# The last 64 channels of convolution and gate, made for two chunks at once in the column halves of the array

## The chip, the cores and the metric

The kernel runs on one core of one Trainium2 chip. The metric is the time of one execution in device microseconds. Durations of single operations come from one profiled execution; the other executions were timed without a profile.

## The reference

Four layers work on `x`, float32, 4 images of 96 channels, 64 x 64 pixels. Layer 0 is a state-space block; the change lies in its first part:

```python
xn = _ln(xp, in_norm_g, in_norm_b)              # tokens of 96 channels
proj = xn @ in_proj_w.T                         # 96 -> 2 * 192
xq, z = jnp.split(proj, 2, axis=-1)
z = _silu(z)                                    # the gate, 192 channels
xc = depthwise_conv_3x3(xq, conv_w)             # 192 channels, 'SAME'
xc = _silu(xc + conv_b)
xs = four directions of xc                      # rows, columns, both flipped
dts, Bs, Cs = split(einsum('bkdl,kcd->bkcl', xs, x_proj_w))
y = selective_scan(xs, dt_proj(dts), A, Bs, Cs, Ds, dt_b)    # 192 channels x 16 states
y = _ln(sum of the four directions of y) * z
x = x + y @ out_proj_w.T
```

Layer 1 is a deformable 3 x 3 convolution (offsets and masks from two convolutions, bilinear samples), layer 2 a Fourier mixer and an MLP with float8 products, layer 3 linear attention and an MLP of the same kind.

## The kernel before

**The scan.** An image is 4096 tokens, cut into 8 chunks of 512 (`CH`, `NCH`). Layer 0's scan runs over units: an image, a direction k, a step of 1024 tokens (two chunks), and 8 channels with their 16 states on the 128 partitions. That makes 1536 units. Each unit has a decay on ScalarE (`decay`, L1014), two bf16 matmuls on TensorE that spread the inflow over the states (`inflow`, L1020), a product on VectorE (L1034), the scan on VectorE (`recur`, L1042), a product on GpSimd (`weigh`, L1051), and its share of a sum over states on TensorE (`total`, L1070). The spread of a unit is issued one unit ahead of its scan, its decay two, the loads of `da` five units ahead (on ScalarE's queue); `du` and `bc` are loaded by SP (L1009, L1000).

**The streams beside it.** All other work is written as generators that yield a `Step` with an estimated time on each engine. `Net`, `Clock`, `pipe` and `Stream` put these steps between the units: a step is issued when the planner's clock says that the engines it needs have room. This happens while the program is built; each engine then has a fixed order of instructions, and at run time waits only for semaphores. There are two streams. The first, `ends`, prepares image 0 (`first`), images 1, 2 and 3 (`before`), and then does layers 2 and 3 image by image (`image`). The second, `middle`, finishes layer 0 behind the scan (`behind`) and does layer 1 with its gathers, also image by image, and is asked first. An image of layers 2 and 3 starts when its samples are there (`net.sampled`). The matmuls of both streams share three PSUM banks (`net.mm`, pool `mm`) while the scan has its own.

**The convolution.** `prepare` multiplies the depthwise weights into the projection, so that a tap of the convolution is a matmul from 96 input channels, over a window of the padded, normed image `pad` that is shifted by the tap. `conv` (L750) makes one chunk: nine taps into one PSUM bank for channels 0 to 127 (g = 0), then nine taps for channels 128 to 191 (g = 1). The second has only 64 channels, so its 64 weight columns stand twice in `w_in` and in the taps' weights, and the sum appears on both halves of the partitions. ScalarE takes the sum through Silu: into `xa` for g = 0 (L773); for g = 1 the lower half into `xc[:64]` in row order (L775), and the upper half into `xc[64:]` in column order (L776). Two gate matmuls follow (L787), for channels 0 to 127 and for 128 to 191, where only 64 of 128 columns are of use; Silu puts them into `zt` (L789), and SP stores z and u (L794 to L796). Silu and the exponential lie in different tables of ScalarE; `exp_and_log` (L411) reloads the latter after each use of Silu.

In `first` (L610) the convolution of chunk j+1 goes beside the projection and the discretisation of chunk j (`projected`, `steps`), in a pipe of six chains; these need the tag `c{j}`, which chunk j's convolution frees when it ends. For images 1 to 3, `inputs` (L690) runs the eight chunks' convolutions in a pipe of two chains, and the rest follows in `before` (L650). `zt` has one buffer for each of its tags; the tag `zt` in the pipe lets one chain at a time be in the gate.

Of the kernel before, what the change touches and what calls it, by code (L numbers as in the profile page):

```python
# [8 lines left out]
F32 = mybir.dt.float32  # L9
# [5 lines left out]
AF = mybir.ActivationFunctionType  # L15
# [539 lines left out]
class Layer0:  # L555
# [54 lines left out]
    def first(self):  # L610
# [5 lines left out]
        with tc.tile_pool(name=f"l0u{b}", bufs=1) as up, tc.tile_pool(name=f"l0b{b}", bufs=1) as sm:  # L616
# [5 lines left out]
            with tc.tile_pool(name=f"l0a{b}", bufs=1) as big, tc.tile_pool(name=f"l0i{b}", bufs=1) as cp:  # L622
# [4 lines left out]
                def rows_first():  # L627
                    yield self.conv(b, 0, pad, us, weights, cp)
                    for j in range(NCH):
                        if j + 1 < NCH:  # L630
                            yield self.conv(b, j + 1, pad, us, weights, cp)
                        yield self.projected(b, j, us, xp_a, xp_c, sm, xdbl, (0,), f"c{j}")
                        for ks in ((0,), (0, 2), (2,)):
                            yield self.steps(b, ks, j, us, dtw, sm, xdbl)
# [55 lines left out]
    def inputs(self, b, up, us):  # L690
# [3 lines left out]
        with tc.tile_pool(name=f"l0a{b}", bufs=1) as big:  # L694
            pad = big.tile([C, PW, PW], F32, name=f"pad{b}", tag="pad")
            yield from self.normed_rows(b, x, pad)
            with tc.tile_pool(name=f"l0i{b}", bufs=1) as sm:
                weights = self.conv_weights(b, sm)
                yield wait(4.0)
                yield from pipe(  # L700
                    self.net, (self.conv(b, j, pad, us, weights, sm) for j in range(NCH)), 2,
                    zt=1, **{f"c{j}": 0 for j in range(NCH)},
                )

# [42 lines left out]
        nc.sync.dma_start(wz, self.net.ins["w_in"][:, 256:])  # L747
        return wc, wz

    def conv(self, b, j, pad, us, weights, sm):  # L750

        net, rows, as_rows = self.net, self.rows, self.as_rows
        nc = net.nc
        wc, wz = weights
        xa, _, xc = us
        xct_v = xc.rearrange("p (w h) -> p h w", h=H)
        cs = slice(j * CH, (j + 1) * CH)
        r0 = j * NR
        for g in range(2):
            pp = net.mm(f"pc{g}_{b}_{j}")  # L760
            for q in range(9):
                dy, dx = divmod(q, 3)
                nc.tensor.matmul(  # L763
                    pp,
                    lhsT=wc[:, q, g * 128 : (g + 1) * 128],
                    rhs=pad[:, r0 + dy : r0 + dy + NR, dx : dx + W],
                    start=(q == 0),
                    stop=(q == 8),
                )
                if q < 8:  # L770
                    yield cost(pe=0.8, holds=1)
            if g == 0:
                nc.scalar.activation(xa[:, cs], pp, AF.Silu, bias=net.vec(V_CBA))  # L773
            else:
                nc.scalar.activation(xc[:64, cs], pp[:64], AF.Silu, bias=net.vec(V_CBC, 64))  # L775
                nc.scalar.activation(  # L776
                    xct_v[64:, r0 : r0 + NR, :],
                    as_rows(pp[64:]),
                    AF.Silu,
                    bias=net.vec(V_CBC, 64, 64),  # L780
                )
            net.exp_and_log()
            yield cost(pe=0.8, act=4.0, new=True, takes="zt" if g else "")
        zts = []
        for g, (c0, n) in enumerate(((0, 128), (128, D2))):
            pz = net.mm(f"pz{g}_{b}_{j}")
            nc.tensor.matmul(pz, lhsT=wz[:, c0 : c0 + 128], rhs=rows(pad, j), start=True, stop=True)  # L787
            zt = sm.tile([128, CH], F32, name=f"zt{g}_{b}_{j}", tag=f"zt{g}")
            nc.scalar.activation(zt[:n], pz[:n], AF.Silu)  # L789
            zts.append((c0, n, zt))  # L790
        net.exp_and_log()
        yield cost(pe=2.0, act=3.8)
        for c0, n, zt in zts:
            nc.sync.dma_start(self.z_d[b][c0 : c0 + n, cs], zt[:n])  # L794
        nc.sync.dma_start(self.u_d[b][:128, cs], xa[:, cs])
        nc.sync.dma_start(self.u_d[b][128:, cs], xc[:64, cs])  # L796
        yield wait(frees=f"zt c{j}")

    def projected(self, b, j, us, xp_a, xp_c, sm, xdbl, qs, takes=""):

# [1120 lines left out]
```

## Time and profile before

| | |
|---|---|
| median of 3 timed executions | 8629.55 us (8617.16 to 8655.84) |
| profiled execution | 8600.48 us |
| its span, first to last instruction | 8598.7 us |
| mean granted TensorE clock | 0.785 of full speed |
| VectorE busy | 6817.9 us (79%) |
| TensorE busy | 6553.4 us (76%) |
| GpSimd busy | 5626.7 us (65%) |
| ScalarE busy | 4945.4 us (58%) |
| first scan starts, last scan ends | 184.97 us, 7551 us |
| convolution's taps (L763) | 568.7 us busy, 1152 records, from 63 to 3588 us |
| gate's matmuls (L787) | 128 records |
| ScalarE's table loads | 201, of 1283 ns each |

In the lines of the profile an entry names the engine (PE is TensorE, PEld its weight load, DVE VectorE, ACT ScalarE, POOL GpSimd, SP the engine that issues most DMAs), the source line, and the tiles written and read. `<-` in a wait names what ended it. A float32 matmul appears as two records. Matmuls are pipelined, so the distance from start to start tells their cost better than their durations. The chain of waits is followed back from the last instruction; here it ends at 3137 us.

### The profile page before, as it was taken

What the parts mean: (1) busy time and instruction counts of PE and PEld (TensorE: products, weight loads), DVE (VectorE), ACT (ScalarE), POOL (GpSimd) and SP (SyncE); (2) the same over time, 40 slices, a digit from 0 to 9 for tenths busy, and PEclk for the clock granted to TensorE, in tenths of its full rate; (3) what the DMA queues carried; (4) which work ended last, traced back from release to release, by engine and by line L of the source; (5) the groups of instructions that cost most, each with busy time, mean ns of one, the idle gap of its engine ahead of it and who ended that gap; (6) DMA issues with size and microseconds to landing.
All of it is one profiled execution on the core that took longest, in us unless ns stands there. A gap on an engine that the chain in (4) does not pass through costs nothing.

```text
span 8598.7 us, 97186 instructions
## 1 busy us (share of the span) xinstructions
PE 6553.4 (76%) x31960; PEld 2840.7 (33%) x31960; DVE 6817.9 (79%) x5118; ACT 4945.4 (58%) x9071; POOL 5626.7 (65%) x4308
## 2 busy tenths in 40 slices
PE   6775877689767668777767888777788776897587
PEld 2211221122222223311223555223455331464374
DVE  2799989888799888688898888888887887838714
ACT  5664666556567668755666667554567765333224
POOL 1565667566579788665688888665787886527700
PEclk8766877779677779876777888676788887798698
DMA  3677678868779889876888989766898887744420
GB/s 97 166 198 195 169 196 220 210 166 201 182 216 243 220 230 226 204 193 181 209 228 223 230 230 229 169 163 166 229 228 226 204 216 180 180 104 137 143 63 13
DMA packets 773932, 1608.32 MB, mean 187 GB/s; under 512 B 264081, under 2 KB 355757, under 8 KB 771222
## 3 DMA queue, kind: packets, MB, share of 16 engines
q10 hardware_dynamic: 244224, 843.17, 38.9%
q1 hardware_dynamic: 455478, 532.37, 24.0%
q0 software_dynamic: 73728, 226.57, 10.1%
q8 instruction: 256, 4.19, 0.2%
q14 instruction: 246, 2.02, 0.1%
HBM read 1345.43 MB, written 256.29 MB: 186 GB/s over the span
## 4 chain that ended last, share of the span: by engine, by line
PE 27%; DVE 14%; DMA 7%; ACT 7%; issue 4%; POOL 2%; ACTq 1%; SPq 1%; DVEq 0%; POOLq 0%
DVE hh L1042 7%; DVE db L1034 3%; PE ps L1416 3%; PE f L1510 3%; PE py L1070 3%; DMA da<-de 2%; PE pd L1432 2%; ACT g L1395 2%; PE db L1020 2%; ACT da L1014 1%; PE h L1551 1%; PE yp L1590 1%; PE zp L1576 1%; POOL hh L1051 1%; PE py L1065 1%
## 5 line engine op out<-in xcount | busy, mean ns | idle before, releaser
L1051 POOL TENSOR_TENSOR hh<-hh,bc 128x1024 f32<-128x1024 f32 x1536 | 3672.1, 2393 | 354.9 <-DVE hh L1042 225.1
L1042 DVE TENSOR_TENSOR_SCAN hh<-da,st,db 128x1024 f32<-128x1024 f32 x1152 | 2700.9, 2345 | 209.5 <-PE py L1070 79.8
L1034 DVE TENSOR_TENSOR db<-db,bc 128x1024 f32<-128x1024 f32 x1536 | 1864.0, 1214 | 610.2 <-PE db L1020 608.7
L1014 ACT ACTIVATE da<-da,w_al 128x1024 f32<-128x1024 f32 x1536 | 1737.6, 1146 | 476.8 <-DMA da<-de 129.9
L1383 POOL DMA_INDIRECT g<-table,idx x1152 | 1201.7, 1043 | 372.3 <-issue 174.8
L1020 PE MATMUL db<-du,rep 24*128 24x512 bf16 x3072 | 700.5, 457 | 780.1 <-DVE hh L1042 748.9
L1070 PE MATMUL py<-hh,w_fold 128*32 128x512 f32 x6144 | 1120.5, 792 | 35.4 <-POOL hh L1051 19.3
L1395 ACT ACTIVATE g<-g,wt 128x96 f32<-128x96 f32 x3456 | 968.3, 364 | 116.7 <-PE py L1070 30.7
L1042 DVE TENSOR_TENSOR_SCAN hh<-da,db 128x1024 f32<-128x1024 f32 x384 | 877.2, 2284 | 73.2 <-PE py L1070 25.1
L1416 PE MATMUL ps<-w_ident,g 128*96 128x128 f32 x3744 | 688.8, 329 | 222.8 <-issue 90.6
L1020 PEld LDWEIGHTS <-rep 24*128 24x128 bf16 x3072 | 159.5, 94 | 1909.3 <-issue 1228.5
L851 POOL TENSOR_TENSOR lw<-lw,w 128x512 f32<-128x512 f32 x192 | 244.0, 1271 | 718.0 <-DVE w L849 686.0
L1416 PEld LDWEIGHTS ps<-w_ident,g 128*96 128x96 f32 x3744 | 499.4, 148 | 568.6 <-ACT g L1395 176.7
L1049 POOL COPY st<-hh 128x1 f32<-128x1 f32 x1152 | 235.1, 204 | 685.3 <-DVE hh L1042 650.5
L763 PE MATMUL pc<-pad,wc 96*128 96x512 f32 x1152 | 568.7, 630 | 6.9 <-ACT st L1424 2.6
L1424 ACT COPY st<-ps 96x384 f32<-96x384 f32 x384 | 180.1, 472 | 543.6 <-PE ps L1416 506.0
L882 PE MATMUL pr<-ex,w_ident 128*128 128x512 f32 x384 | 294.7, 859 | 147.6 <-DVE ex L872 58.6
L840 PE MATMUL pd<-xd,w_dtw 103*64 103x512 f32 (+1 forms) x512 | 279.0, 820 | 68.1 <-DVE rl L853 30.4
L1432 PE MATMUL pd<-st,wdc 96*128 96x256 f32 x1152 | 320.5, 430 | 11.4 <-ACT st L1424 4.8
L763 PEld LDWEIGHTS pc<-pad,wc 96*128 96x128 f32 x1152 | 217.1, 199 | 308.7 <-issue 289.2
L1070 PEld LDWEIGHTS py<-hh,w_fold 128*32 128x32 f32 x6144 | 160.5, 125 | 387.4 <-issue 293.6
L1519 ACT COPY d<-f 128x512 f32<-128x512 f32 x192 | 111.2, 581 | 299.7 <-PE f L1510 287.5
(253 smaller groups left out, 8940.0 us busy)
## 6 DMA issues: line engine op xcount, KB each, us to landing
da<-de ACTq DMA_DIRECT2D x1536, 512.0 KB
du<-du SPq DMA_DIRECT2D x1536, 96.0 KB
bc<-bcd SPq DMA_DIRECT2D x128, 512.0 KB
y<-yb SPq DMA_DIRECT2D x384, 128.0 KB
de<-rl SPq DMA_DIRECT2D x128, 256.0 KB
m<-in_dft SPq DMA_DIRECT2D x128, 256.0 KB
ad<-y ACTq DMA_DIRECT2D x192, 128.0 KB
table<-pix SPq DMA_DIRECT2D x256, 96.0 KB
```

Source lines behind the costliest of these rows:

```text
L763: nc.tensor.matmul(pp, lhsT=wc[:, q, g * 128 : (g + 1) * 128], rhs=pad[:, r0 + dy : r0 + dy + NR, dx : dx + W], start=(q == 0), stop=(q == 8),
L882: nc.tensor.matmul(pr, lhsT=net.ident, rhs=ex, start=True, stop=False)
L1014: self.net.nc.scalar.activation(u.da, u.da, AF.Exp, scale=self.al[:, a : a + 1])
L1020: self.net.nc.tensor.matmul(db[:, h, :], lhsT=self.rep[64 * u.q + 32 * h : 64 * u.q + 32 * h + 24], rhs=u.du[64 * u.q + 32 * h : 64 * u.q ...
L1034: self.net.nc.vector.tensor_mul(u.db, u.db, u.bc[:, 0, :])
L1042: nc.vector.tensor_tensor_scan(u.along(u.hh), u.along(u.da), u.along(u.db), first, ALU.mult, ALU.add)
L1051: self.net.nc.gpsimd.tensor_mul(u.hh, u.hh, u.bc[:, 1, :])
L1070: nc.tensor.matmul(py[p0 : p0 + 32], lhsT=self.fold[:, u.i, :], rhs=hc[:, h * CH : (h + 1) * CH], start=u.sums["add"] is None and u.i == 0 ...
L1383: nc.gpsimd.indirect_dma_start(out=g[:, k, :], out_offset=None, in_=self.tables[b % 2], in_offset=bass.IndirectOffsetOnAxis(ap=idx[:, n : ...
L1395: nc.scalar.activation(pixel, pixel, AF.Identity, scale=wt[:, n, c : c + 1])
L1416: nc.tensor.matmul(pt[:, k, :], lhsT=g[:, k, c * C : (c + 1) * C], rhs=net.ident, is_transpose=True, start=(c == 0), stop=(c == corners - 1),)
L1432: nc.tensor.matmul(po, lhsT=wdc[:, k, :], rhs=st[:, k, :], start=(k == 0), stop=(k == 8))
```

## The change

`conv` now makes a pair of chunks. The 128-channel part is done as before, for one chunk and then for the other. For the last 64 channels the weights are used once: each tap is two matmuls with 64 columns, the first chunk's sum on partitions 0 to 63 and the second chunk's on 64 to 127 of the same bank, that is, one in each column half of the array. Two activations then read each half, one for the row order and one for the column order. The gate's last 64 channels are made in the same way, and one activation takes both halves. The planner's costs of these steps are changed with it, `first` and `inputs` count pairs, the second chunk's gate has a tile of its own, and both chunks' tags are freed together. Their z and u are stored in one group of eight DMAs.

```diff
@@ first
                 def rows_first():
                     yield self.conv(b, 0, pad, us, weights, cp)
                     for j in range(NCH):
-                        if j + 1 < NCH:
-                            yield self.conv(b, j + 1, pad, us, weights, cp)
+                        if j % 2 == 0 and j + 2 < NCH:
+                            yield self.conv(b, j // 2 + 1, pad, us, weights, cp)
@@ inputs
-                    self.net, (self.conv(b, j, pad, us, weights, sm) for j in range(NCH)), 2,
+                    self.net, (self.conv(b, jp, pad, us, weights, sm) for jp in range(NCH // 2)), 2,
@@ conv
-    def conv(self, b, j, pad, us, weights, sm):
+    def conv(self, b, jp, pad, us, weights, sm):
 
         net, rows, as_rows = self.net, self.rows, self.as_rows
         nc = net.nc
         wc, wz = weights
         xa, _, xc = us
         xct_v = xc.rearrange("p (w h) -> p h w", h=H)
-        cs = slice(j * CH, (j + 1) * CH)
-        r0 = j * NR
-        for g in range(2):
-            pp = net.mm(f"pc{g}_{b}_{j}")
+        pair = (2 * jp, 2 * jp + 1)
+        key = f"{b}_{jp}"
+
+        def shifted(j, q):
+            dy, dx = divmod(q, 3)
+            return pad[:, j * NR + dy : j * NR + dy + NR, dx : dx + W]
+
+        for j in pair:
+            pp = net.mm(f"pc0_{b}_{j}")
             for q in range(9):
-                dy, dx = divmod(q, 3)
                 nc.tensor.matmul(
-                    pp,
-                    lhsT=wc[:, q, g * 128 : (g + 1) * 128],
-                    rhs=pad[:, r0 + dy : r0 + dy + NR, dx : dx + W],
+                    pp, lhsT=wc[:, q, :128], rhs=shifted(j, q), start=(q == 0), stop=(q == 8)
+                )
+                if q < 8:
+                    yield cost(pe=0.8, holds=1)
+            nc.scalar.activation(xa[:, j * CH : (j + 1) * CH], pp, AF.Silu, bias=net.vec(V_CBA))
+            net.exp_and_log()
+            yield cost(pe=0.8, act=2.0, new=True)
+        pp = net.mm(f"pc1_{key}")
+        for q in range(9):
+            for i, j in enumerate(pair):
+                nc.tensor.matmul(
+                    pp[64 * i : 64 * i + 64],
+                    lhsT=wc[:, q, 128:192],
+                    rhs=shifted(j, q),
                     start=(q == 0),
                     stop=(q == 8),
                 )
-                if q < 8:
-                    yield cost(pe=0.8, holds=1)
-            if g == 0:
-                nc.scalar.activation(xa[:, cs], pp, AF.Silu, bias=net.vec(V_CBA))
-            else:
-                nc.scalar.activation(xc[:64, cs], pp[:64], AF.Silu, bias=net.vec(V_CBC, 64))
-                nc.scalar.activation(
-                    xct_v[64:, r0 : r0 + NR, :],
-                    as_rows(pp[64:]),
-                    AF.Silu,
-                    bias=net.vec(V_CBC, 64, 64),
-                )
-            net.exp_and_log()
-            yield cost(pe=0.8, act=4.0, new=True, takes="zt" if g else "")
+            if q < 8:
+                yield cost(pe=0.8, holds=1)
+        for i, j in enumerate(pair):
+            half, bias = pp[64 * i : 64 * i + 64], net.vec(V_CBC, 64, 64 * i)
+            nc.scalar.activation(xc[:64, j * CH : (j + 1) * CH], half, AF.Silu, bias=bias)
+            nc.scalar.activation(xct_v[64:, j * NR : (j + 1) * NR, :], as_rows(half), AF.Silu, bias=bias)
+        net.exp_and_log()
+        yield cost(pe=0.8, act=4.2, new=True, takes="zt")
         zts = []
-        for g, (c0, n) in enumerate(((0, 128), (128, D2))):
-            pz = net.mm(f"pz{g}_{b}_{j}")
-            nc.tensor.matmul(pz, lhsT=wz[:, c0 : c0 + 128], rhs=rows(pad, j), start=True, stop=True)
-            zt = sm.tile([128, CH], F32, name=f"zt{g}_{b}_{j}", tag=f"zt{g}")
-            nc.scalar.activation(zt[:n], pz[:n], AF.Silu)
-            zts.append((c0, n, zt))
+        for j in pair:
+            pz = net.mm(f"pz0_{b}_{j}")
+            nc.tensor.matmul(pz, lhsT=wz[:, :128], rhs=rows(pad, j), start=True, stop=True)
+            zt = sm.tile([128, CH], F32, name=f"zt{j % 2}_{b}_{j}", tag=f"zt{j % 2}")
+            nc.scalar.activation(zt, pz, AF.Silu)
+            zts.append(zt)
+        pz = net.mm(f"pz1_{key}")
+        for i, j in enumerate(pair):
+            nc.tensor.matmul(
+                pz[64 * i : 64 * i + 64], lhsT=wz[:, 128:192], rhs=rows(pad, j), start=True, stop=True
+            )
+        zc = sm.tile([128, CH], F32, name=f"zt2_{key}", tag="zt2")
+        nc.scalar.activation(zc, pz, AF.Silu)
         net.exp_and_log()
-        yield cost(pe=2.0, act=3.8)
-        for c0, n, zt in zts:
-            nc.sync.dma_start(self.z_d[b][c0 : c0 + n, cs], zt[:n])
-        nc.sync.dma_start(self.u_d[b][:128, cs], xa[:, cs])
-        nc.sync.dma_start(self.u_d[b][128:, cs], xc[:64, cs])
-        yield wait(frees=f"zt c{j}")
+        yield cost(pe=3.0, act=4.5)
+        for i, j in enumerate(pair):
+            cs = slice(j * CH, (j + 1) * CH)
+            nc.sync.dma_start(self.z_d[b][:128, cs], zts[i])
+            nc.sync.dma_start(self.z_d[b][128:, cs], zc[64 * i : 64 * i + 64])
+            nc.sync.dma_start(self.u_d[b][:128, cs], xa[:, cs])
+            nc.sync.dma_start(self.u_d[b][128:, cs], xc[:64, cs])
+        yield wait(frees=f"zt c{pair[0]} c{pair[1]}")
```

## The prediction

> **What bounds the kernel now.** I read the page first, then busy times by stretch, VectorE's waits, the convolution's own lines, the chain of waits in one convolution stage, and the order in time around one pair of half-width matmuls.
>
> The first scan (L1042) starts at 184.97 us and the last ends at 7551: 1536 units of 4.8 us. Before lie image 0's norm and first chunks, behind lie 1048 us of image 3's last stages. Stretches (columns: busy us of each engine, TensorE clock, DMA): the scan phase, and the convolutions of images 1, 2 and 3.
>
> ```profile
> core 0: us, PE busy (x) PEld busy (x) DVE busy (x) ACT busy (x) POOL busy (x), PEclk, DMA share, GB/s
> 185.00:7551.00 7366.00, 5617.16 (x25964) 2244.70 (x25964) 6275.75 (x4295) 4532.11 (x8308) 5243.82 (x3981) 0.77 0.80 203
> ...
> 940.00:1150.00 210.00, 195.55 (x628) 68.65 (x632) 183.38 (x106) 149.95 (x146) 128.08 (x82) 0.95 0.73 186
> 1840.00:2150.00 310.00, 283.03 (x886) 87.38 (x884) 261.88 (x162) 193.93 (x206) 199.85 (x135) 0.92 0.82 196
> 3300.00:3600.00 300.00, 271.95 (x1164) 118.44 (x1160) 228.08 (x134) 258.25 (x507) 234.25 (x180) 0.96 0.86 221
> ```
>
> Over the whole phase VectorE is busiest (6276 of 7366, 85%). In the three convolution stages it is TensorE: 93%, 91%, 91%, VectorE 87%, 84%, 76%. VectorE's idle time in the scan phase (last two numbers: times, longest):
>
> ```profile
> DVE db L1034 <- PE db L1020: 584.4, 278, 29.1
> DVE hh L1042 <- PE py L1070: 104.9, 98, 5.9
> DVE hh L1042 <- ACT da L1014: 29.6, 20, 3.8
> ```
>
> So TensorE late with the spread inflow is what VectorE waits for. In image 3's stage (3290 to 3610) the chain of waits runs over the convolution; it is traced back to 3137 us only, so the earlier stages can't be read so.
>
> ```profile
> by line: PE pc L763 22.8%; PE ps L1416 8.3%; ACT g L1395 7.9%; DVE hh L1042 7.3%; ACT da L1014 6.9%; PE py L1070 5.8%; PE pd L1432 5.4%; ACT L413 4.4%; issue 4.2%; DVE db L1034 3.8%; PE db L1020 3.7%; DMA wc<-wc_d 3.1%; PE py L1065 2.8%; AC
> ```
>
> 22.8% of 320 us is 73 us of taps, and 4.4% is 14 us of reloading the exponential table (L413). The price of a pair of half-width matmuls, in order of time (start, us):
>
> ```profile
> 137.48 3.60 PE L763 MATMUL pc<-pad,wc 96*128 96x512 f32 x8
> 140.91 1.02 PE L882 MATMUL pr<-ex,w_ident 128*128 128x512 f32 x2
> ...
> 143.07 1.88 PE L763 MATMUL pc<-pad,wc 96*128 96x512 f32 x4
> 144.97 1.08 PE L840 MATMUL pd<-xd,w_dtw 103*64 103x512 f32 x4
> 145.98 1.55 PE L763 MATMUL pc<-pad,wc 96*128 96x512 f32 x3
> ```
>
> One fp32 matmul is two records. Eight records take 140.91-137.48 = 3.43 us from start to start, so 0.86 us a matmul: call that a slot. The two 64-column matmuls of `pd`, in different column halves, take 145.98-144.97 = 1.01 us together, not 1.72; they overlap. The four records before them take 1.90 instead of 1.72. Going into half columns and out again so costs 0.18+0.15 = 0.33 us.
>
> **What the Trainium skill says.** "TensorEngine Tiling (Array Packing)", Key Properties: tiles of one mode run independently, but a change of mode drains TensorE. The trace agrees with both (1.01 us for two; 0.33 us a change). "TensorE: Matmul & The Clock Gate", Part 3, table of measured speedups: three column tiles of 32 gave 2.38 times. Here the offset convolution, over the same shifted windows, does better with four: 18 matmuls (36 records) in 5.28 us are 0.29 us each, 2.9 times.
>
> ```profile
> 7651.46 5.28 PE po L1278 x36
> ```
>
> "ScalarE: Activation LUTs", What ACT_TABLE_LOAD costs: 1283 ns, and 1380 ns of drain. The loads are 1.283 us here, but the next instruction follows at once (an activation ends at 72.01, load at 72.02, next load at 73.31), so I count no drain. "PSUM — Partial Sum Buffer", Engine vs sequencer instructions: matmuls start and end in program order; so a matmul waiting for a bank holds all behind it. The same bears on the last rival below.
>
> **The change, part by part, for a pair of chunks** (16 pairs).
>
> *TensorE.* Before: 36 tap and 4 gate matmuls, 40 slots, 34.4 us. After: 18 taps of 128 channels, 9 slots of two half-width taps, 2 gates and 1 shared gate slot, 30 slots, 25.8 us: 8.6 us less. In the order of the changed program the half-width taps stand in 46 runs and the shared gates in 16; 62 changes of 0.33 us are 20 us, 1.3 us a pair. Left: 7.3 us a pair, 117 us in all.
>
> *ScalarE.* Before: 12 table loads of 1.283 (15.4 us), 2 x 0.687 + 2 x 0.682 + 2 x 1.145 + 4 x 0.590 = 7.4 us. After: 8 loads (10.3 us), one gate activation less (6.8 us). 5.7 us a pair, 91 us in all.
>
> *VectorE, GpSimd, DMA.* Same operations, same bytes. The eight stores of z and u leave in one go behind the last gate; SP waited 226 us for the gate before (36 times), now half as often and longer. Behind it on SP stand the scan's du and bc loads, which are issued at least five units (some 24 us) before their use; eight issues of about 0.5 us are covered. If that cover went, each of twelve groups could cost what exceeds it: 0 to 5 us, so 60 us at most. I take 0.
>
> *Before the first scan.* Projection of chunk 0 stands behind 48 slots instead of 41 (+6 us); from there to the first spread there are 30 instead of 39 convolution slots (-8 us) and 44 instead of 51 us of ScalarE work. I take 0, bounds -8 and +8. But 42 slots are left for the scan phase instead of 80.
>
> *Planned order.* The planner's cost of a half-width step is still 0.8 us for two overlapping taps. So convolution 1 stands beside units 146-173 instead of 151-194, convolution 3 beside 579-628 instead of 650-706, and image 3's last preparation at unit 795 instead of 889. Fourier and MLP work of image 1 then ends at unit 1426, not 1473; image 2 can't follow, since its samples come at unit 1472 in both orders. So half the lead is spent waiting, VectorE's total work beside the scan is the same, and the 1048 us behind the scan are the same work in the same order.
>
> *What that is worth, by stage.* Four pairs save 29 us of TensorE an image. Image 3: VectorE has room (228 of 300); of the 80 us of taps and gates on the chain 7.3/34.4 go, 17 us, and a quarter of the 32 us of ScalarE's convolution work on it, 8: 25 us. Image 2: room too, VectorE 262 of 310: 18 us. Image 1: 183 of 210 is nearly VectorE's limit, 12 us. Image 0: 156 us from 185 to 341, where VectorE is busy 107 and TensorE 117: mostly latencies, 10 us of the 33 us that leave. Sum 65; of this I give back 10 for the wait at unit 1426, where the scan runs a little quicker but has nothing to fill. **-55 us.** A second way: cutting the scan phase into stretches of 16 units and fitting their length to the work of TensorE and VectorE in them gives 0.27 us per us of TensorE and 0.97 per us of VectorE: 134 us of slots less are then -41 with an error of 15. I keep -55, since these fits mix stages where TensorE has room.
>
> **Rivals.**
>
> *VectorE is the bound, and TensorE's time goes idle.* For it: 85% busy over the phase; in the convolution stages the waits for `db` are no denser than elsewhere. Against it: 91 to 93% TensorE there and the chain. Time: 0 to -15 us, 8615 to 8630.
>
> *The halves don't overlap, or the changes of mode eat the gain.* Then 40 slots as before, planned as 30: -0, and late spreads, say 8640. Against it: 1.01 us for two.
>
> *The gate takes its banks in one step, and it gets slower.* The pool has three banks; the changed gate step asks for three at once (two before), while the half-width sum is still being read (1.28 + 2 x 1.83 = 4.9 us) and the other chain holds a third bank. TensorE then stands until ScalarE has read the sum, reloaded (1.28), loaded (1.28) and copied the first gate (0.59); the next unit's spread is queued behind. The inflow is one unit early, so the first 4 us are covered. To come out slower by 0.5% each of 16 pairs must cost VectorE (55+43)/16 = 6 us. For it: ScalarE's queue also carries decays and sampling. Against it: all waits of the gate's matmuls now are about 70 us for 64. Where it decides, +60 us: 8690. Another order of everything beside the scan, with its chances both ways (a stretch of 16 units scatters by 8 us around the fit), belongs to the range.
>
> **How the numbers follow.** The profiled execution took 8600.48 us, 1.8 more than its span; the median of the runs shown is 8629.55, 0.34% more, so 55 us stay 55. 8629.55-55 = **8575**. Chances: the forecast 0.55 (own range 8535 to 8610; 0.46 of it beyond 0.5%, below 8586, and 0.09 short of it), VectorE's bound 0.20 (no change), no overlap 0.05 (0.03 none, 0.02 slower), gate 0.20 (0.03 none, 0.17 slower). About 0.5% is what a measurement tells here from no change: 8617 to 8656 is the scatter. Faster 0.46, same 0.35, slower 0.19. Range 8500 to 8690: the planner's reshuffle below, the gate above.
>
> **What would show it.** Half-width taps: pairs start 0.86 to 0.9 us apart inside a run. ScalarE busy about 91 us less, TensorE 100 to 120. First scan at 177 to 193. Convolution stages with VectorE above 88%. Last scan near 7500, 1048 us behind it unchanged. If the gate's matmuls wait for ScalarE by over 100 us in all, or spreads make VectorE wait by more than 584 us, the last rival holds. Wrong altogether if the scan's units outside the convolution stages change their pace.

## The result, and the profile after

The changed kernel takes 8689.4 us, median of 20 executions (8652.27 to 8724.51); the kernel before, run beside it, 8638.25 us (20 executions). The ratio is 1.0059, 95% interval 1.0045 to 1.0073: slower by 0.6%, where 0.6% faster was forecast. The profiled execution's span is 8659.5 us, its mean granted TensorE clock 0.773 (before: 8598.7 us, 0.785).

The first section of the page, busy time of each engine, of the kernel after:

```profile
PE 6445.4 (74%) x31938; PEld 2783.5 (32%) x31960; DVE 6814.1 (79%) x5118; ACT 4855.5 (56%) x8991; POOL 5606.8 (65%) x4308
```

Against 6553.4 and 4945.4 us before, TensorE works 108 us less (99 to 134 between the two profiles taken of each kernel) and ScalarE 90 us less, nearly what was forecast (100 to 120, and 91). So the work did leave. In the stretches view the scan phase comes first, then the convolutions of images 1, 2 and 3, each from the first chunk's activation into `xa` to the last chunk's:

```profile
core 0: us, PE busy (x) PEld busy (x) DVE busy (x) ACT busy (x) POOL busy (x), PEclk, DMA share, GB/s
192.00:7565.00 7373.00, 5495.84 (x25930) 2181.56 (x25952) 6273.52 (x4296) 4447.62 (x8233) 5235.82 (x3981) 0.76 0.79 203
938.00:1074.00 136.00, 123.20 (x416) 38.28 (x414) 94.72 (x55) 85.51 (x85) 68.06 (x51) 0.90 0.60 161
1743.00:1930.00 187.00, 177.77 (x597) 50.22 (x595) 145.89 (x89) 114.90 (x124) 117.33 (x92) 0.90 0.74 191
3085.00:3314.00 229.00, 203.38 (x877) 78.51 (x877) 171.66 (x101) 175.52 (x344) 176.08 (x151) 0.88 0.82 214
```

The scan phase is as long as before (7373 against 7366 us) with the same VectorE time in it (6274 against 6276). The convolutions are over sooner, but VectorE is busy in only 70, 78 and 75% of them, against 87, 82 and 75% in the same stretches of the kernel before (its second profile, `before_again` below): they now stand beside 27, 39 and 48 scan units instead of 43, 62 and 57. TensorE fills 91, 95 and 89% of these shorter stages, at a granted clock of about 0.9, so the time that left it was not filled with scan units. In the chain of waits over image 3's stage (3060 to 3340 us) the taps (L767 and L778) still make 20.4% of 280 us, 57 us, against 73 before:

```profile
by line: PE pc L767 11.7%; PE pc L778 8.7%; DMA da<-de 8.0%; PE ps L1434 7.8%; ACT g L1413 7.6%; PE py L1088 6.6%; PE pd L1450 6.4%; DVE hh L1060 6.0%; PE db L1038 4.8%; PE py L1083 4.5%; issue 3.6%; ACT L413 3.2%; ACTq L1011 3.0%; ACT da L
```

VectorE's waits (total, times, longest) answer the three lines of before:

```profile
DVE db L1052 <- PE db L1038: 575.4, 251, 23.2
...
DVE hh L1060 <- PE py L1088: 93.6, 83, 5.0
...
DVE hh L1060 <- ACT da L1032: 13.0, 16, 1.9
```

The wait for the spread (`db`) is 575 us where it was 584: no difference for the whole (the second profiles of both kernels have 599 and 596), but in units 144 to 192, where image 1's convolution lies, it is 53 us in the changed kernel and 14 before. What is new is in TensorE's own waits, at the shared gate (L802):

```profile
PE pz L802 <- ACT zt L798: 46.6, 10, 7.2
...
PE pz L802 <- ACT xa L772: 4.8, 2, 2.6
```

In order of time (start, us; in brackets the wait just ahead of it), two groups of full-width matmuls for comparison, two runs of half-width taps of image 1, and the gate that follows:

```profile
935.97 1.98 PE L767 MATMUL pc<-pad,wc 96*128 96x512 f32 x4
...
942.16 1.07 PE L1088 MATMUL py<-hh,w_fold 128*32 128x512 f32 x8
...
952.06 3.65 PE L778 MATMUL pc<-pad,wc 96*64 96x512 f32 x16
...
955.96 4.51 PE L778 MATMUL pc<-pad,wc 96*64 96x512 f32 x20
...
961.72 1.13 PE L767 MATMUL pc<-pad,wc 96*128 96x512 f32 x2
...
963.10 2.31 PE L796 MATMUL pz<-pad,wz 96*128 96x512 f32 x4
964.25 1.28 ACT L413 ACT_TABLE_LOAD   x1
965.54 2.19 ACT L1032 ACTIVATE da<-da,w_al 128x1024 f32<-128x1024 f32 x2
967.75 1.28 ACT L798 ACT_TABLE_LOAD   x1
969.04 1.08 ACT L798 ACTIVATE zt<-pz 128x512 f32<-128x512 f32 x2
969.69 1.98 PE L802 MATMUL pz<-pad,wz 96*64 96x512 f32 x4 [4.28 <-ACT zt L798]
971.60 3.78 PE L767 MATMUL pc<-pad,wc 96*128 96x512 f32 x4
...
975.32 0.60 PE L1038 MATMUL db<-du,rep 24*128 24x512 bf16 x2
975.85 1.94 PE L1088 MATMUL py<-hh,w_fold 128*32 128x512 f32 x8
977.71 2.58 PE L767 MATMUL pc<-pad,wc 96*128 96x512 f32 x4
```

The half-width taps do overlap: 20 records are ten matmuls, five pairs, 0.89 us a pair from start to start. Then two plain gate matmuls take two banks at 963.10. The next pair's taps hold the third (L767 at 961.72, sum not finished), so the shared gate can only have the bank of the first gate matmul, and that is read only after a reload of the exponential table, two decays and the load of Silu's table: the first of the two copies at 969.04 ends about 969.6, and TensorE starts 0.1 us later, having stood 4.28 us, in which no other matmul ran. After that it is slow: four records take 3.78 us (1.98 at 935.97), eight of `py` 1.94 (1.07 at 942.16). From start to start the work from 969.69 to 980.22 is about 4.4 us longer than at the usual pace, so this wait takes twice its length of TensorE. "TensorE: Matmul & The Clock Gate", Part 1, says the clock falls to half after an idle window of about 3.4 us; the trace agrees here: its record of the granted clock stands at half from 968.70 us, 3.3 us into the wait, for 10.24 us. (`third_bank` below shows that less is enough.)

### The profile page after: what moved, and what is told of

It reads as the page before. It is cut to its first block, busy times and chain, and to the rows that moved or that the text cites. A ratio compares the mean times of both kernels' runs of the same rounds, so it can differ in the third digit from the quotient of the medians.

```text
span 8659.5 us, 97118 instructions
## 1 busy us (share of the span) xinstructions
PE 6445.4 (74%) x31938; PEld 2783.5 (32%) x31960; DVE 6814.1 (79%) x5118; ACT 4855.5 (56%) x8991; POOL 5606.8 (65%) x4308
## 4 chain that ended last, share of the span: by engine, by line
PE 35%; DVE 30%; DMA 11%; ACT 9%; issue 8%; POOL 2%; ACTq 1%; SPq 1%; another core or an unknown queue 0%; DVEq 0%; POOLq 0%
DVE hh L1060 15%; DVE db L1052 8%; PE py L1088 4%; PE ps L1434 4%; DMA da<-de 3%; PE f L1528 3%; PE pd L1450 3%; PE pc L767 2%; ACT g L1413 2%; PE db L1038 2%; ACT da L1032 2%; PE py L1083 1%; PE pc L778 1%; ACTq L1011 1%; POOL hh L1069 1%
## 5 line engine op out<-in xcount | busy, mean ns | idle before, releaser
L1434 PE MATMUL ps<-w_ident,g 128*96 128x128 f32 x3744 | 716.5, 341 | 242.2 <-issue 110.0
L767 PE MATMUL pc<-pad,wc 96*128 96x512 f32 x576 | 297.4, 652 | 3.8 <-ACT zt L798 2.7
L1450 PEld LDWEIGHTS pd<-st,wdc 96*128 96x128 f32 x1152 | 245.2, 221 | 100.3 <-issue 43.1
```

The source lines that it names most:

```text
L767: nc.tensor.matmul(pp, lhsT=wc[:, q, :128], rhs=shifted(j, q), start=(q == 0), stop=(q == 8))
L1434: nc.tensor.matmul(pt[:, k, :], lhsT=g[:, k, c * C : (c + 1) * C], rhs=net.ident, is_transpose=True, start=(c == 0), stop=(c == corners - 1),)
L1450: nc.tensor.matmul(po, lhsT=wdc[:, k, :], rhs=st[:, k, :], start=(k == 0), stop=(k == 8))
```

## The experiments

The theories named in the expectations: S, TensorE stands at the third bank of the shared gate and then runs at a lower clock; V, VectorE bounds the scan phase, and TensorE's time is worth nothing; T, the loss lies behind the last scan (1094.5 us in the profile after, 1047.7 before); later Q, the planner's costs are too low and squeeze the convolution; J, any change of the planned order moves the time. Ratios are to the kernel before on the same chip; its medians there were 8664.62 us (runs up to `e_gate_split`), 8661.18 (up to `v_early_costs`), 8657.36 (up to `early_over`), 8658.38 (up to `before_down`) and 8603.28 (the last two).

### The changed kernel again, and without its third bank

`after_again` is the changed kernel as it is.

> The changed kernel a second time, for a second profile. Theory T with a cause in the order: again some 1090 us behind the last scan, and TensorE gaps of 9 to 15 us late in image 3's sampling. If those were chance: 1045 to 1060 us. Theory S: again some 50 us of TensorE waits at the shared gate and 60 us more VectorE idle time in units 144 to 192 and 576 to 624.

8706.77 us, 1.0047 [1.0028, 1.0065]. The waits at L802 are 55 us again, and VectorE waits 57 us for `db` in units 144 to 192, as S said; behind the last scan lie 1081 us.

`e_two_banks`, from the changed kernel, leaves out the shared gate's matmuls, so that the last 64 channels of z are not computed; the activation reads the second gate's sums instead:

```diff
-        pz = net.mm(f"pz1_{key}")
-        for i, j in enumerate(pair):
-            nc.tensor.matmul(
-                pz[64 * i : 64 * i + 64], lhsT=wz[:, 128:192], rhs=rows(pad, j), start=True, stop=True
-            )
```

> The changed kernel with the shared gate's two half-width matmuls left out; its activation reads the second gate's sums instead (the last 64 channels of z are not computed). Planned costs and the order of all other instructions stay those of the changed kernel, so only the request for a third bank goes, and 0.9 us of TensorE a pair. Theory S (TensorE stands at the third bank, 12 times 4.3 us, and runs at half clock after it): the convolution stages speed up, VectorE waits 60 us or more less for db, ratio to the kernel before 0.995 to 1.000. Theory V (VectorE bounds the scan phase, TensorE's time is worth nothing there): 1.005 to 1.006, as the changed kernel. Theory T (the loss lies behind the last scan): 1.005 too, with some 1090 us behind the last scan.

8632.36 us, 0.9961 [0.9945, 0.9976]: 74 us less than the changed kernel in the same group, in the same planned order. What was left out of TensorE is 16 pairs of 1.06 us and the changes of mode, some 22 us; at the worth of TensorE's time that the next run gives (0.37) this is 8 us. So about 66 us are the stall's, for 55 us of waits (an estimate; the two intervals together leave some 20 us either way). VectorE's wait for `db` is 540 us, 35 and 59 less than in the two profiles of the changed kernel, where S expected 60 or more. Its three convolution stretches:

```profile
941.00:1053.00 112.00, 110.67 (x416) 35.90 (x416) 95.54 (x56) 84.16 (x84) 68.55 (x52) 1.00 0.71 189
1724.00:1904.00 180.00, 171.70 (x589) 49.36 (x589) 146.64 (x89) 114.62 (x125) 118.03 (x92) 0.91 0.79 199
3050.00:3272.00 222.00, 193.75 (x865) 78.00 (x864) 172.53 (x102) 175.58 (x344) 180.12 (x154) 0.89 0.86 226
```

Image 1's convolution takes 112 us instead of 136, at a full clock (1.00 instead of 0.90). Of the 24 us, 11.5 are idle time of TensorE (12.8 us in the changed kernel, nearly all at banks, 1.3 here) and 12.5 its work: 3 us are the three shared gates in that stretch (3 x 1.06), the rest is other work that takes longer. In images 2 and 3 it is 7 us each, so these stages hold about half of the 74 us; where the rest goes one profile of each doesn't say. The four waits in image 0 (21 us) cost nothing that shows: at unit 140 both profiles of the changed kernel are level with this one within 6 us.

### Less TensorE work, nothing else

`e_fewer_taps`, from the kernel before, leaves out seven of the nine taps for the last 64 channels:

```diff
-                nc.tensor.matmul(
+                if g == 0 or q in (0, 8):
+                    nc.tensor.matmul(
```

> The kernel before, with seven of nine taps of the last 64 channels' convolution left out (these channels get a wrong sum). The steps are still yielded with their planned costs, so the order stays that of the kernel before, and 7 x 32 slots of 0.86 us, 193 us, leave TensorE, more than the change takes away. My prediction's conversion (0.27 to 0.45 us of time per us of TensorE): -50 to -85 us, ratio 0.990 to 0.994. Theory V: ratio 0.998 to 1.000.

8593.79 us, 0.992 [0.9901, 0.9939]. It removes 32 x 7 x 0.86 = 193 us of TensorE (the last 64 channels get only two taps) and gives 71: 0.37 us per us. V falls: in a fixed order TensorE's time in these stages counts.

### The shared gate in a step of its own

`e_gate_split`, from the changed kernel:

```diff
             zts.append(zt)
+        net.exp_and_log()
+        yield cost(pe=2.0, act=3.8, new=True)
         pz = net.mm(f"pz1_{key}")
...
-        yield cost(pe=3.0, act=4.5)
+        yield cost(pe=1.0, act=3.2)
```

> The changed kernel, with the shared gate in a step of its own behind the other two gates (two table loads more a pair), so that two banks are asked for at a time and other work comes between. All is computed. Theory S: ratio 0.995 to 1.000, waits of the shared gate's matmuls for the first gate's activation down from 51 us to under 20. Theory V or T: 1.003 to 1.008, the order's chance.

8637.23 us, 0.997 [0.9954, 0.9985]. With the whole change made, and two table loads more for a pair, but no third bank asked for, it is faster than before. The gates' matmuls wait 6 us in all, and image 1's convolution runs at a clock of 1.00.

### The stall alone, in the kernel before

`before_again` is the kernel before, for its profile.

> The kernel before, once more, on the chip of the other runs, for its profile. Theory T (the loss lies behind the last scan) needs the stretch behind the last scan to be near 1048 us again, against 1081 to 1105 us in the five other profiles. If it is 1080 us or more here, that difference lies between profiles and not between kernels, and T falls. The phase from the first scan to the last should be about 7370 to 7400 us at a granted clock near 0.77.

8668.95 us; behind the last scan lie 1093 us, so T falls: the 1048 us of the first profile were that execution's. `third_bank`, from the kernel before, with its order and costs:

```diff
             zts.append((c0, n, zt))
+        p3 = net.mm(f"p3_{b}_{j}")
+        nc.tensor.matmul(p3[:, :8], lhsT=wz[:, :128], rhs=pad[:, j * NR + 1, 1:9], start=True, stop=True)
+        z3 = sm.tile([128, 8], F32, name=f"z3_{b}_{j}", tag="z3")
+        nc.scalar.activation(z3, p3[:, :8], AF.Silu)
```

> The kernel before with the suspected cause and nothing else of the change: the gate of each chunk asks for a third bank in its step, for one matmul of 8 columns, which ScalarE takes at the end; costs and order as before. It adds about 32 x 0.1 us of TensorE and 32 x 0.25 us of ScalarE. Theory S (TensorE stands at the third bank until the gate's first sum is taken): TensorE waits about 4 us at that matmul in most of the 32 gates, 80 to 130 us in all, and the kernel is slower by 0.6 to 1.6%. Theory V (VectorE bounds, TensorE's time is worth nothing): within 0.2% of before.

8717.1 us, 1.007 [1.005, 1.009]: 56 us for a third bank asked for in 32 gates, with next to no work. The time is what S said, the waits are not: 36 us at the small matmul, where 80 to 130 were expected (16 of its 22 waits are under 1.2 us), and 12 us at taps that take a bank after it (L763). TensorE's waits, then the convolution stretches of `before_again` and of `third_bank`:

```profile
PE p L792 <- ACT zt L789: 29.9, 19, 6.4
...
PE pc L763 <- ACT zt L789: 11.9, 4, 4.2
```

```profile
955.00:1127.00 172.00, 165.49 (x541) 57.85 (x541) 149.90 (x87) 129.23 (x126) 104.55 (x62) 0.97 0.74 192
1849.00:2130.00 281.00, 255.28 (x795) 77.23 (x793) 231.29 (x143) 173.23 (x184) 180.26 (x121) 0.92 0.80 196
3299.00:3570.00 271.00, 249.41 (x1036) 108.61 (x1035) 202.75 (x119) 230.47 (x452) 210.98 (x161) 0.93 0.83 217
```

```profile
965.00:1161.00 196.00, 178.96 (x554) 63.42 (x552) 150.75 (x87) 130.42 (x133) 104.88 (x62) 0.92 0.66 173
1880.00:2184.00 304.00, 278.98 (x810) 85.28 (x809) 232.53 (x143) 174.35 (x191) 180.47 (x121) 0.84 0.75 181
3354.00:3637.00 283.00, 254.68 (x1036) 110.06 (x1035) 198.88 (x117) 231.29 (x459) 207.55 (x158) 0.91 0.79 207
```

The same stages are 24, 23 and 12 us longer, with the same VectorE work, and the clock falls in each: 0.97 to 0.92, 0.92 to 0.84, 0.93 to 0.91. So it is shown in two fixed orders, once by taking the cause away and once by adding it, that asking for a third bank costs about as much time as the change lost. (Both edits also shift which of the three banks later tiles get; no run parts this from the request itself.)

How it costs is not quite as S has it. In image 2's stage of `third_bank` TensorE stands no longer than before (304.00 - 278.98 = 25.0 us against 281.00 - 255.28 = 25.7), and its waits at the small matmul there are 0.2 to 0.7 us; but for some 2 us of small matmuls, the 23 us more are the same work at a lower clock. So no wait near 4 us is needed for the clock to fall, nor the idle window of 3.4 us named above. The clock's record goes in steps of 3.41 us. In the scan phase of `third_bank` (200 to 7500 us), of the steps at full clock in which TensorE's records, whose ends are modelled, leave it idle for under 1.0 us, 18 of 739 are followed by half clock; with 1.0 to 1.8 us 105 of 213; with more 218 of 222 (`before_again`: 20 of 741, 99 of 207, 203 of 205). So a short wait counts where others fall beside it.

### The shared gate earlier, and the planner's costs

`v_early` moves the shared gate into the step of the last pair of half-width taps, which holds one bank and asks for a second; the table loads stay at eight:

```diff
+        pz = net.mm(f"pz1_{key}")
+        for i, j in enumerate(pair):
+            nc.tensor.matmul(pz[64 * i : 64 * i + 64], lhsT=wz[:, 128:192], rhs=rows(pad, j), start=True, stop=True)
         for i, j in enumerate(pair):
             half, bias = pp[64 * i : 64 * i + 64], net.vec(V_CBC, 64, 64 * i)
...
+        nc.scalar.activation(zc, pz, AF.Silu)
         net.exp_and_log()
-        yield cost(pe=0.8, act=4.2, new=True, takes="zt")
+        yield cost(pe=1.8, act=4.8, new=True)
```

> The changed kernel with the shared gate moved up into the step of the half-width taps' last pair, which holds one bank and so asks for no third; the table loads stay eight for a pair, two fewer than with the gate in a step of its own. S: no wait of over 1 us in most gates, 0.4 to 0.6% faster than before (0.35% with the gate in a step of its own, and 41 us of ScalarE less). V: within 0.2% of the changed kernel.

8659.96 us, 0.9998 [0.9978, 1.0018]. The gates' matmuls wait 10 us in all, but there is no gain: a miss for S alone. `v_early_costs` gives the planner what the trace shows, 1.283 + 0.687 + 1.283 = 3.3 us of ScalarE for the step that the change entered at 2.0:

```diff
-            yield cost(pe=0.8, act=2.0, new=True)
+            yield cost(pe=0.9, act=3.3, new=True)
...
-                yield cost(pe=0.8, holds=1, takes="zt" if q == 7 else "")
+                yield cost(pe=1.0, holds=1, takes="zt" if q == 7 else "")
...
-        yield cost(pe=1.8, act=4.8, new=True)
+        yield cost(pe=2.3, act=6.9, new=True)
```

> The same, with the planner told what the steps take by the trace: 3.3 us of ScalarE for the 128-channel step (2.0 before), 1.0 us for a pair of half-width taps (0.8), 6.9 us for the step with the halves and the shared gate (4.8). If the planner's low costs squeeze the convolution into too few units (in the profiles without the stall the units 144 to 192 still take 36 us more than before), this is another 10 to 25 us faster than without, and VectorE's idle time there falls back from 38 us towards 22. If the squeeze costs nothing, it is the same within 0.15%.

8608.27 us, 0.9936 [0.9911, 0.9961]: 52 us faster than `v_early`, more than twice what was expected. So the costs, or the order that they make, count, and Q had to be told from J. `after_true_costs` sets the same costs in the changed kernel and leaves its gate alone (`act` 2.0 to 3.3, 4.2 to 6.3, 4.5 to 4.4, half-width `pe` 0.8 to 1.0, the 128-channel step's 0.8 to 0.9).

> The changed kernel with nothing altered but the planner's costs, set to what the trace shows: 128-channel step 3.3 us of ScalarE (2.0), a pair of half-width taps 1.0 us (0.8), the halves' step 6.3 us of ScalarE (4.2), gate 4.4 (4.5). The stall at the third bank stays. Theory Q (the change told the planner too little, so it squeezes the convolution into too few units): 0.3 to 0.6% faster than the changed kernel, so 0.999 to 1.003 of before, with the waits at the shared gate still near 50 us. If only the stall counts: as the changed kernel, 1.004 to 1.006.

8659.13 us, 1.0006 [0.9987, 1.0026]. Within what Q said, but the waits at L802 fell too, to 21 us, so it doesn't tell the two apart. `split_true_costs` does the same to `e_gate_split`.

> Shared gate in its own step (no stall, two more table loads for a pair) with the same true costs. Q: 0.992 to 0.995 of before, against 0.997 with the low costs. If the low costs do no harm: 0.996 to 0.998 again.

8629.71 us, 0.9967 [0.995, 0.9984], as with the low costs: against Q. `early_jitter` changes two low costs of `v_early` by a trifle:

```diff
-            yield cost(pe=0.8, act=2.0, new=True)
+            yield cost(pe=0.8, act=2.2, new=True)
...
-        yield cost(pe=1.8, act=4.8, new=True)
+        yield cost(pe=1.8, act=5.0, new=True)
```

> The shared gate moved up, with two low costs changed by a trifle (2.0 to 2.2, 4.8 to 5.0 us of ScalarE). It tells how much any new order moves the time (theory J: what the true costs gained was one lucky order among many). Q: 0.998 to 1.001, as without the trifle (0.9998). J: anywhere from 0.993 to 1.003.

8584.12 us, 0.9896 [0.987, 0.9922], below even J's range. `early_over` has costs a fifth above the trace's.

> The shared gate moved up, with costs about a fifth above those of the trace (ScalarE 4.0, 8.2 and 4.5 us). Q: as with the true costs, 0.991 to 0.996, since the convolution is spread at least as far. J: anywhere from 0.993 to 1.003.

8586.1 us, 0.9917 [0.9889, 0.9945]: what Q said, and below J's range. But Q falls as a rule: `split_true_costs` gained nothing, and `early_jitter`, with costs nearly as low as in `v_early`, does no worse than the true ones. What is left is J, with a wider spread than it stated: one kernel in four orders takes 0.9896 to 0.9998 of before.

### The same trifle in the other kernels

> The fastest kernel so far once more: shared gate moved up, costs 2.2 and 5.0 us. If 0.9896 of six executions is its time: 0.988 to 0.992. If it was a chance of few executions: 0.993 to 0.997.

8585.71 us, 0.9917 [0.989, 0.9943]: the gain is real. `after_jitter` is the changed kernel with `act` 2.0 to 2.2 and 4.2 to 4.4.

> The changed kernel with the same trifle in two costs (2.0 to 2.2, 4.2 to 4.4 us of ScalarE); the shared gate asks for its third bank as before. S alone: 1.003 to 1.007 of before, as 1.0059 and 1.0047 in the first order. J (order luck): anywhere from 0.994 to 1.008; below 0.999 would say that the loss was the order's as much as the stall's.

8642.34 us, 0.9987 [0.9973, 1.0]: against S alone, and just below the mark under which the loss was to be called the order's as much as the stall's. The order moved the stall too: its waits at L802 are 32 us instead of 52. `before_up` and `before_down` are the kernel before with one cost changed:

```diff
-            yield cost(pe=0.8, act=4.0, new=True, takes="zt" if g else "")
+            yield cost(pe=0.8, act=4.2, new=True, takes="zt" if g else "")
```

> The kernel before with the convolution's ScalarE cost at 4.2 instead of 4.0 us; the same instructions in another order. If the order of the kernel before is an ordinary one: within 0.3% of it, on either side. If it was a lucky one: 1.003 to 1.008. J: a spread like that of the four orders with the shared gate moved up (0.9896 to 0.9998).

8584.97 us, 0.9917 [0.9885, 0.9948].

> The same with 3.8 instead of 4.0 us; the same expectations. Both runs on one side of before would say that its order is lucky or unlucky; one on each side that the order's part averages out.

8603.9 us (3.8 instead of 4.2), 0.994 [0.9916, 0.9963]. So of three orders of the kernel before its own is the slowest: a trifle in a cost gives it 54 to 73 us, as much as the whole change was forecast to bring.

### What in the order counts

In the traces, the orders differ in where image 2's Fourier work begins, counted by the scan unit beside which its first product on VectorE (`d`) stands. Before the last two runs it began at unit 1485 to 1488 in all five orders that do the whole work and are faster than 0.995 (and in `after_true_costs`), and at 1489 to 1491 in the others. From unit 1488 to the end the first kind took 1258 to 1301 us, the second 1288 to 1340. This mark was found in the runs that it sorts, and it is one unit wide: by the first Fourier transform itself (`f`) `before_up`, `before_down` and the changed kernel all begin at unit 1495. Two runs move this start, and with it what follows; everything planned before it stays in place. `after_end_soon` leaves out two of the planner's waits in the changed kernel, so that it begins at 1484 instead of 1489:

```diff
-    yield wait(max(0.0, end - clock.now()))
+    yield wait(max(0.0, end - clock.now()) * (lane is not SOON))
...
-            yield from pipe(self.net, chains, 8, g=6, st=1, xo=1)
+            yield from pipe(self.net, chains, 8, lane=SOON if b == 2 else None, g=6, st=1, xo=1)
...
-            yield wait(4.0)
+            yield wait(4.0 * (b != 2))
```

> The changed kernel with image 2's Fourier work planned at unit 1484 instead of 1489: the planner's two waits ahead of it are left out; every instruction before that is where it was. If the start of image 2's Fourier work is what sets the fast and the slow orders apart: 20 to 50 us faster than the changed kernel, 0.999 to 1.003 of before, and the stretch from unit 1488 to the end 1260 to 1300 us instead of 1310 to 1320. If it is not: 1.004 to 1.007, as the changed kernel.

8625.46 us, 1.003 [1.0015, 1.0044], and 1260 us from unit 1488 on. `early_end_late` delays it in the order of `early_jitter` (`yield wait(4.0 + 40.0 * (b == 2))`).

> The fastest order (shared gate moved up, costs 2.2 and 5.0 us) with image 2's Fourier work planned at unit 1490 instead of 1486 by a wait of 40 us in the planner's clock; all before that unchanged. If that start counts: 0.994 to 0.998 of before, against 0.9896 and 0.9917, and 1300 to 1330 us from unit 1488 to the end instead of 1258 to 1272. If it does not: 0.989 to 0.993.

8608.55 us, 1.0004 [0.999, 1.0018], and 1291 us from unit 1488 on, against 1258 and 1272; in the traces' count its start is 1489 instead of 1485. Stretches from unit 1488 to the last scan and behind it, of `early_jitter_again` and of `early_end_late`:

```profile
7314.48:7530.29 215.81, 183.11 (x1548) 112.11 (x1545) 190.23 (x130) 94.13 (x127) 140.48 (x89) 0.90 0.79 189
7530.29:8572.80 1042.51, 806.57 (x5631) 542.60 (x5629) 503.85 (x757) 314.28 (x634) 374.93 (x313) 0.84 0.33 92
```

```profile
7299.21:7533.36 234.15, 190.42 (x1547) 111.16 (x1547) 192.59 (x134) 90.30 (x120) 141.60 (x89) 0.83 0.69 166
7533.36:8590.20 1056.84, 819.33 (x5744) 551.75 (x5742) 508.85 (x762) 319.52 (x641) 373.62 (x313) 0.83 0.32 92
```

With the late start the last 48 units run at a clock of 0.83 instead of 0.90 and take 18 us more, and 113 more matmul records are left behind the last scan. Both runs moved the way the start says, the first by as little as was expected of it (its interval still touches that of `after_again`), the second by more (0.994 to 0.998 was expected). The size isn't settled. These two ran on a chip on which the kernel before took 8603 us, not some 8660, and no other kernel ran on both. `early_end_late` is slower than `early_jitter` by 0.9 to 1.1% in ratios, but by 23 to 24 us in microseconds, and by 19 to 33 us from unit 1488 on; `after_end_soon` is faster than the changed kernel by 0.2 to 0.3% in ratios, but by 64 to 81 us in microseconds.

All together, by that start and by TensorE's waits at a third bank (us):

| kernel | image 2's Fourier begins | waits | ratio |
|---|---|---|---|
| before | 1491 | | 1 |
| `before_up`, `before_down` | 1488 | | 0.9917, 0.994 |
| `third_bank` | 1491 | 36, and 12 at taps | 1.007 |
| changed, twice | 1489 | 52, 55 | 1.0059, 1.0047 |
| `after_jitter` | 1489 | 32 | 0.9987 |
| `after_true_costs` | 1487 | 21 | 1.0006 |
| `after_end_soon` | 1484 | 54 | 1.003 |
| without the stall: `e_gate_split`, `split_true_costs`, `v_early`, `early_end_late` | 1489 | 0 | 0.997, 0.9967, 0.9998, 1.0004 |
| `v_early_costs`, `early_over`, `early_jitter` twice | 1485 | 0 | 0.9936, 0.9917, 0.9896, 0.9917 |

Among orders with the late start, the change without the stall stands at 0.9985 (mean of four) against 1; among those with the early start, at 0.992 (mean of three kernels) against 0.993. So over these orders the change without its stall shows a worth of 0 to 0.2%, no more than the intervals are wide. The shared gate moved up, with costs 2.2 and 5.0, is faster than the kernel before by 0.8 to 1.0% and than the changed kernel by 1.3 to 1.6%; but the kernel before with a cost of 4.2 is as fast.

## Why the prediction was wrong

**Right.** A slot of 0.86 us and overlapping halves (0.89 us a pair); TensorE 108 us less, ScalarE 90 us less; the first scan at 192.6 us, at the end of 177 to 193; the worth of TensorE's time, 0.37 in a fixed order, between the 0.27 of the second way and the 0.47 that 55 us for 117 us come to, where ScalarE's part is in it. The stretch behind the last scan shows no change: 1048 and 1093 us in the two profiles of before, 1095 and 1081 in those of the changed kernel. The time lies inside the stated range, at its upper end.

**The step that failed** is the third bank: the sum of -55 us has no term for it, and the rival "The gate takes its banks in one step" was put at 0.20 because "all waits of the gate's matmuls now are about 70 us for 64". Those waits belong to a gate that asks for two banks; they say nothing of one that asks for three. (The 70 us also count the idle time of the weight loads; its matmuls themselves waited 27 us.) The rival described the event rightly: the other chain's bank, the reload, the load, the first copy. But its price took the wait as all there is, "the first 4 us are covered" by the spread issued a unit ahead. The runs showed that idle time of TensorE is also followed by a lower clock, on which all that comes after pays again: 55 us of waits were worth about 66 us, and 36 to 48 us in `third_bank` were worth 56. So the thresholds under "What would show it" could not show it: the gate's waits are 52 and 55 us, not over 100, and VectorE's for `db` are 575 and 599 us, on both sides of 584. That the rival's 8690 us is the time measured, to 1 us, is luck: it stands on 8630 for the kernel before, which took 8638 here, and its 60 us were not worked out from waits.

**Mis-sized** is the gain itself. Forecast and result are 106 us apart, and the stall is some 66 of them. Without the stall and in nearly the same order the change gave 24 to 27 us (`e_gate_split`; `e_two_banks` less 8 us for what it leaves out), not 55, and 0 to 0.2% over several orders. Why it is worth so little is not shown. The second way under "What that is worth" came nearer than the sum, and nearer than it says itself: 134 x 0.27 is 36 us, not 41.

**Wrong too, with less weight.** VectorE was to fill the convolution stages above 88%; it fills 70 to 78%. The stages move beside fewer units (27 instead of 43 for image 1), as the planned order had said, so TensorE bounds them as before and the time saved is not spent on units there. The last scan was to end near 7500 us and ends at 7565 and 7606. "Image 2 can't follow" took its start as fixed: it moves by a few units with trifles, and two runs show that this moves the time.

**Left out of the sum** is the order. The prediction gave "another order of everything beside the scan" a place in the range only. Runs of the kernel before in two other orders were faster by 0.6 and 0.8%, so one order of each kernel can't tell a change of 0.6% from luck. The stall is told from it because `e_two_banks` and `third_bank` keep their orders.

**Open.** Which other parts of the order count beside image 2's start, and how much of the 0.9% between `early_jitter` and `early_end_late` belongs to the chip; and whether the change is worth anything over many orders. One thing points to the clock: over the timed executions beside the experiments its mean is 0.781 to 0.785 for the kernel before and 0.787 in its two other orders, but 0.770 to 0.780 in every kernel with the change, with the stall or without, and 0.772 in `e_fewer_taps`, which only leaves taps out. Where TensorE had less to do, its clock was lower; no run shows how much of the saved time goes that way.

## What to carry to other kernels

When an edit puts one more PSUM tile into a step, count the banks that other chains hold at that moment, and ask which engine must finish what, behind which table loads, before the bank comes free: the in-order engine stands for all of that. Price a stall of TensorE by more than its length: here 1.2 to 1.6 us per us of wait in all, nothing that shows in image 0, and twice for the one wait followed through. Count the short waits near it too, since it was the idle time within some 3.4 us that went with a fall of the clock. Before a forecast below 1% is believed of a kernel whose order a planner makes, move a cost by a trifle in both kernels and look at the spread; a cause is best shown in a kernel whose order stays as it is.

## What was not expected of the hardware

One wait of 4.28 us was followed by 8.6 us in which float32 matmuls took nearly twice their time (four records 3.78 us, elsewhere 1.98), and a stage without such waits was granted a clock of 1.00 where the same work with 13 us of them had 0.90. Waits much shorter than 3.4 us did the same where several fell together: of the 3.41 us steps with more than 1.8 us of idle time, 218 of 222 were followed by half clock, and half of those with 1.0 to 1.8 us. Asking for a bank for eight columns of output, some 0.5 us of work on TensorE and ScalarE, cost 1.75 us a gate (56 us over 32).
